# A bottleneck-attention block in fp32: four silus change places with the copies of the projection behind them

## The chip, the cores and the metric

The kernel runs on one core of a Trainium2 chip. The metric is the device time of one execution in microseconds, taken as the median of several runs. The core has five engines that each work through their own queue in order: TensorE (PE in the profile, with its weight loads apart as PEld), VectorE (DVE), ScalarE (ACT), GpSimd (POOL) and SyncE (SP, which issues DMAs). An instruction that has to wait for another engine waits on a semaphore, and everything behind it on its own queue waits with it.

## The reference

The input `x` has 8 samples of 512 channels of 32 x 32 pixels, in fp32. It is group-normed and sent through a block with two attention stages. The result is added to `x`. `cbs` is a convolution, a batch norm with fixed statistics and a silu.

```python
t = cbs(x, cv1_w, cv1_bn, 0)                     # 1x1, 512 -> 512
ys = [t[:, :C], t[:, C:]]                        # C = 256
for i in range(2):
    yi = ys[-1]
    z = cbs(yi, m_cv1_w[i], m_cv1_bn[i], 1)      # 3x3, 256 -> 256
    z = bot_attention(z, m_qkv_w[i], m_rw[i], m_rh[i])
    z = silu(bn_eval(conv2d(z, m_cv2_w[i], 0), m_cv2_bn[i]))
    ys.append(yi + z)
return cbs(concatenate(ys, axis=1), cv2_w, cv2_bn, 0)

def bot_attention(x, qkv_w, rw, rh):             # 4 heads of 64 channels, 1024 positions
    q, k, v = conv2d(x, qkv_w, 0) split in three
    logits = q . (k + rw + rh) * 64 ** -0.5
    return softmax(logits) . v
```

## The kernel before, in words

The eight samples are worked through in four pairs (loop variable `p`, 0 to 3). For each pair the program runs, stage by stage: the first 3x3 convolution (n = 0) on both samples together, then for each sample the projection to q, k and v and the attention, then the 1x1 convolution behind it; the same again with n = 1; and the closing 1x1 convolution. While the attention runs, pieces of the next pair's work are slipped in between. The order of the instructions on each engine is fixed when the program is built; `tc.issue_after(ins)` in the source ties an instruction behind another one of the same engine, and where no such tie stands a scheduler sets the order. Waits between engines are worked out from the tiles that instructions read and write.

**The 3x3 convolution** (`conv3x3`) is a Winograd transform. It runs over two blocks of 128 output channels (`oc`), and for each over three steps (`i`). In each step TensorE forms products into the PSUM tile `c3_ps` (L653), ScalarE copies part of them (L658), and VectorE turns them back into pixels. In the last step of the last block (`oc` = 1, `i` = 2), that VectorE work is cut in three parts: the first half of the pixels of the first sample, its second half, and the whole of the second sample. Each part ends with L714 and L715, which write the pixels into the tile `z`. Behind them stand silus on ScalarE (L719, recorded at L495), each in place on 512 pixels of `z`: one for the first part, one for the second, two for the third. I call these four **S1, S2, S3 and S4**. S1 makes the block called `b21` in the projection, S2 makes `b22`; S3 and S4 belong to the second sample, whose projection comes only after the first sample's attention.

**The projection** (`project_strassen`) forms q, k and v of one sample by seven products of blocks (Strassen-Winograd). A product is named by its weight: 11, s1, 12, s4, s2, s3, 22. Each has a part for q and k (L926, two matmuls of 512 columns, shown as x4 in the trace) and a part for v (L932, four matmuls of 128 columns, shown as x8). PSUM tiles collect them:

- product 11 (on `b11`) and product 12 (on `b21`) are summed in `ps_a` and in the first half of `ps_v`;
- product s1 (on `t1`) and product s4 (on `b22`) are summed in `ps_b` and in the second half of `ps_v`;
- s2 (on `t2`), s3 (on `t3`) and 22 (on `t4`) go to fresh tiles.

Before product 12 may be added onto product 11, the value of product 11 alone has to be saved, and the same for s1 and s4. That is what four ScalarE copies do: `u_z` (L968, from `ps_a`), `m_z` (L969, from `ps_b`), `u_zv` and `m_zv` (L971 and L972, from the two halves of `ps_v`). After products 12 and s4, five more copies bring out finished blocks: `q` and `vT` (L978, L980), then `kr`, `q` and `vT` (L983, L984, L985), and a table load for exp follows (L510), since the attention's exponentials come next on ScalarE. VectorE meanwhile makes `t2`, `t3`, `t4` from the blocks of `z` (L973 to L975), adds the position terms to k (L956), and later combines the products (L991 to L1016). The order of the matmuls on TensorE is 11 and s1 (q and k), 11 and s1 (v), 12 (q and k), 12 (v), s4 (q and k), s4 (v), s2, s3, 22, and then the attention's logits.

The tiles `q` and `kr` take over buffers that the convolution's VectorE work reads until its end (`c3_t` and `c3_k`, tags "q" and "k"), so their first writes wait for that work: the first `q` copy waits for L705 of the third part.

`project_strassen` is called with `table=True` right behind a convolution, for the first sample of a pair. This happens seven times: behind the convolution n = 0 of the pairs 1 to 3, and behind n = 1 of all four pairs. In pair 0 the first projection is another function (`project_direct`). The second sample's projections (`table` not set) have no convolution right ahead of them.

Of the kernel before, what the change touches and what calls it, by code (L numbers as in the profile page):

```python
# [61 lines left out]
def kernel(  # L62
# [16 lines left out]
    nc = tc.nc  # L79
# [5 lines left out]
    NM = C // P  # L85
# [8 lines left out]
    G = 2  # L94
# [396 lines left out]
    def stages(act, small, ps_big, ps_av, n_pt):  # L491
# [117 lines left out]

        def conv3x3(n, vs, u_of, z, groups=G, summed=None, after=None, between={}):  # L610

# [9 lines left out]
            for oc in range(NM):  # L621
                dst = z[:, oc].rearrange("p g x -> p (g x)").rearrange("p (t r w) -> p r t w", r=4, w=F)
                for i in range(NI):
# [57 lines left out]
                    for (at, size), m in zip(parts, m_parts):  # L681
# [31 lines left out]
                        if final:  # L713
                            stt(dst[:, 0, tl], tiles(r0), -6.0, tiles(big_s[:, xs_]), ALU.mult, ALU.add)  # L714
                            read = stt(dst[:, 3, tl], tiles(r1), -6.0, tiles(big_d[:, xs_]), ALU.mult, ALU.add)  # L715
                            for block in range(at // half_q, (at + size) // half_q):
                                g, half = divmod(block, NH)
                                z_part = z[:, oc, g, ts(half, HALF)]
                                last_silu = silu(z_part, z_part, bn_m1[n] + oc)  # L719
            if summed is None:  # L720
# [191 lines left out]

        def project_strassen(n, z, w, t, early=None, middle=None, table=False):

# [31 lines left out]
            def v_of(ap):  # L946
                return ap.rearrange("p (j o) -> p j o", o=P)
# [20 lines left out]
            nc.scalar.copy(u, ps_a)  # L968
            nc.scalar.copy(m5, ps_b)  # L969
            to_v(ps_v[:, 1], w["s1"], t1)  # L970
            nc.scalar.copy(u_v, ps_v[:, 0])  # L971
            nc.scalar.copy(m5_v, ps_v[:, 1])  # L972
            tt(t2, b22, t1, ALU.subtract)  # L973
# [10 lines left out]
            nc.scalar.copy(q1, ps_b[:, 0])  # L984
            copied = nc.scalar.copy(v1, v_of(ps_v[:, 1]))  # L985
            if table:
# [998 lines left out]
    for p in range(NP):  # L1985
        ia, ib = G * p, G * p + 1
        more = p + 1 < NP
        direct = p == 0
# [57 lines left out]
        def direct_keys(which):  # L2046
# [5 lines left out]
        }  # L2052
        z = new_z()
        t = s.conv3x3(
            0, vs, u_of(0), z, summed=None if direct else z[:, :, 0], after=last_out,
            between=in_first if direct else {},
        )
# [19 lines left out]
        else:  # L2077
            qkv = s.project_strassen(0, z[:, :, 0], take_blocks("sq", 0, 0, SQ_NAMES), t, table=True)

# [230 lines left out]
        z = new_z()  # L2310
        t = s.conv3x3(1, vs, u_of(1), z, summed=z[:, :, 0])
        feed(sqs(1, 1))
        w = take_blocks("sq", 1, 0, SQ_NAMES)
        qkv = s.project_strassen(1, z[:, :, 0], w, t, table=True)

# [269 lines left out]
```

## Time and profile before

| | |
|---|---|
| median of 3 runs | 2235.71 us (2235.07 to 2235.83) |
| the profiled execution | 2234.68 us, its span 2233.2 us |
| TensorE busy | 2192.9 us, 98% of the span |
| VectorE busy | 1752.3 us, 78% |
| ScalarE busy | 1094.0 us, 49% |
| GpSimd busy | 225.1 us, 10% |
| granted TensorE clock, mean | 0.998 of full speed |

The span is the time between the first and the last instruction in the trace; the device time has 1.5 us around it. In a row of the timeline stand the start in us from the span's start, the duration in us, the engine, the line, the operation, the tile written and the tiles read, the shapes and how many instructions are merged in the row. A bracket at the end gives the idle time of that engine just before the row and what ended it. Matmuls are pipelined: the next one starts a little before the row of the one ahead of it ends. ScalarE's and VectorE's instructions overlap in the same way by about 0.1 us.

The seven calls behind a convolution can be found by the start of their `u_z` copy: 374, 672, 923, 1219, 1468, 1764 and 1991 us. Of these 672, 1219 and 1764 stand behind n = 0, the other four behind n = 1.

### The profile page before, as it was taken

Reading aid. Unit: us, or ns where it says so; the run is one execution under the profiler, and the core shown is the slowest. Engines: PE = TensorE matmul, PEld = TensorE weight load, DVE = VectorE, ACT = ScalarE, POOL = GpSimd, SP = SyncE. Lnnn points to the kernel's source line nnn. Section 1 sums busy time; section 2 is a strip of 40 time slices with the busy share of each in tenths; the row PEclk is TensorE's granted clock in tenths of the full one; section 3 lists DMA queues with packets and bytes.
Section 4 is the critical chain, followed back from the end, with each engine's and each line's share of the span. In section 5 each row is a group of like instructions: output and inputs, shape, how many; then the busy total and the mean of one; then the engine's idle time right before and its main releaser. Section 6 shows DMA issues by size and latency. Waiting matters only on the chain.

```text
span 2233.2 us, 40366 instructions
## 1 busy us (share of the span) xinstructions
PE 2192.9 (98%) x16330; PEld 1079.5 (48%) x16330; DVE 1752.3 (78%) x2794; ACT 1094.0 (49%) x1324; POOL 225.1 (10%) x417
## 2 busy tenths in 40 slices
PE   7999999999999999999999999999999999999998
PEld 3653437343474444734447443564344834373433
DVE  7988879878669688986858868997794877897664
ACT  7554553644225666356323576445622455336543
POOL 3322210000220000000021000000002100000001
PEclk9999999999999999999999999999999999999999
DMA  9854447321582323612268141542126701251123
GB/s 271 307 170 140 162 149 258 109 74 52 141 256 73 103 97 121 209 49 77 58 155 272 34 156 44 180 140 77 58 67 170 267 30 44 91 202 39 58 58 96
DMA packets 133798, 285.61 MB, mean 128 GB/s; under 512 B 33540, under 2 KB 61184, under 8 KB 132580
## 3 DMA queue, kind: packets, MB, share of 16 engines
q1 hardware_dynamic: 101700, 197.34, 26.7%
q0 software_dynamic: 31904, 85.61, 13.2%
q8 instruction: 131, 2.15, 0.4%
q14 instruction: 63, 0.52, 0.1%
HBM read 214.86 MB, written 68.03 MB: 127 GB/s over the span
## 4 chain that ended last, share of the span: by engine, by line
PE 83%; DVE 12%; ACT 2%; issue 1%; DMA 1%; POOL 0%; SPq 0%; DVEq 0%; ACTq 0%; POOLq 0%
PE av_ps L1081 18%; PE l_ps L1047 17%; PE c L1315 9%; PE c_new L1315 8%; PE c_ps L653 8%; PE p_ps L926 5%; PE m_ps L1295 5%; PE x_ps L1555 4%; PE ps L523 3%; PE p_ps L932 3%; DVE acc L1067 2%; PE s_ps L1099 1%; PE p_ps L896 1%; DVE c_e L694 1%; DVE c_r L703 1%
## 5 line engine op out<-in xcount | busy, mean ns | idle before, releaser
L1051 ACT ACTIVATE pt<-l_ps 128x1024 f32<-128x1024 f32 x512 | 495.5, 1023 | 336.5 <-PE l_ps L1047 218.9
L1067 DVE TENSOR_TENSOR acc<-acc,pt 128x1024 f32<-128x1024 f32 x384 | 469.7, 1223 | 44.2 <-ACT pt L1051 17.2
L1081 PE MATMUL av_ps<-pt,vT 64*64 64x512 f32 x4096 | 484.9, 590 | 4.9 <-DVE z L1089 4.6
L1047 PE MATMUL l_ps<-q,kr 64*64 64x512 f32 x4096 | 486.1, 590 | 2.3 <-ACT pt L1051 1.2
L1081 PEld LDWEIGHTS av_ps<-pt,vT 64*64 64x64 f32 x4096 | 156.3, 133 | 284.4 <-issue 233.5
L1047 PEld LDWEIGHTS l_ps<-q,kr 64*64 64x64 f32 x4096 | 157.6, 133 | 272.2 <-issue 247.3
L653 PEld LDWEIGHTS c_ps<-v_in,u 128*64 128x64 f32 x4320 | 235.8, 137 | 6.4 <-issue 6.1
L653 PE MATMUL c_ps<-v_in,u 128*64 128x128 f32 x4320 | 238.6, 273 | 0.1
L1295 PE MATMUL m_ps<-z,m_sb 128*128 128x512 f32 x256 | 113.8, 592 | 0.0
L658 ACT COPY c_m<-c_ps 128x512 f32<-128x512 f32 x48 | 28.1, 585 | 166.7 <-PE c_ps L653 148.4
L1089 DVE TENSOR_TENSOR z<-av_ps,z 128x512 f32<-128x512 f32 x64 | 44.1, 690 | 80.6 <-ACT z L1088 80.6
L926 PE MATMUL p_ps<-t_z,sq 128*128 128x512 f32 x224 | 105.9, 595 | 0.0
L495 ACT ACTIVATE t<-m_ps,bh,sh 128x512 f32<-128x512 f32 x64 | 46.3, 774 | 93.8 <-PE m_ps L1295 92.6
L1065 DVE TENSOR_TENSOR acc<-pt 128x1024 f32<-128x1024 f32 x64 | 78.0, 1219 | 16.7 <-PE s_ps L1099 11.2
L926 PE MATMUL p_ps<-z,sq 128*128 128x512 f32 x168 | 81.0, 602 | 0.7 <-ACT z L495 0.7
L1295 PEld LDWEIGHTS m_ps<-z,m_sb 128*128 128x128 f32 x256 | 47.9, 190 | 56.5 <-issue 51.4
L495 ACT ACTIVATE z<-z,bh,sh 128x512 f32<-128x512 f32 x64 | 48.6, 806 | 36.3 <-DVE z L715 36.3
L1157 DVE TENSOR_TENSOR z<-z,rs 128x512 f32<-128x512 f32 x64 | 42.4, 687 | 25.2 <-DMA rs<-r_dram 25.1
L932 PEld LDWEIGHTS p_ps<-sq,z 128*128 128x128 f32 x336 | 43.3, 191 | 28.7 <-ACT m_zv L972 14.0
L926 PEld LDWEIGHTS p_ps<-t_z,sq 128*128 128x128 f32 x224 | 39.5, 191 | 36.5 <-issue 34.4
L1555 PE MATMUL x_ps<-t_x,sw 128*128 128x512 f32 x128 | 55.9, 592 | 0.0
L1315 PE MATMUL c_new<-t_in,wss 128*128 128x512 f32 x128 | 55.9, 592 | 0.0
(341 smaller groups left out, 3137.3 us busy)
## 6 DMA issues: line engine op xcount, KB each, us to landing
u<-u SPq DMA_DIRECT2D x135, 512.0 KB
y_in<-y SPq DMA_DIRECT2D x32, 512.0 KB
rs<-r_dram SPq DMA_DIRECT2D x126, 128.0 KB
sq<-sq SPq DMA_DIRECT2D x42, 384.0 KB
x<-in_x_dram SPq DMA_DIRECT2D x28, 512.0 KB
r_in<-r SPq DMA_DIRECT2D x28, 512.0 KB
c_out<-in_x_dram POOLq DMA_DIRECT2D x56, 256.0 KB, 5.1
out_dram<-c_out POOLq DMA_DIRECT2D x56, 256.0 KB, 3.7
```

Source lines behind the costliest of these rows:

```text
L495: silued[0] = nc.scalar.activation(dst, src, AF.Silu, scale=sh[:, k : k + 1], bias=bh[:, k : k + 1])
L653: conv_product[0] = nc.tensor.matmul(to[o], us[cp][:, k, row, c, o], rhs, start=(k == 0), stop=(k == NM - 1),)
L926: nc.tensor.matmul(ps[:, o, :], w[:, o, :], rhs, start=not onto, stop=True, skip_group_check=onto)
L932: nc.tensor.matmul(v[:, ts(j, P)], rhs[:, ts(j, P)], w[:, 2, :], start=j == 0 and not onto, stop=True, skip_group_check=True,)
L1047: nc.tensor.matmul(ps[kh * HD : (kh + 1) * HD, hd, :], kr[r, c, o : o + HD], q[r, c, ts(half, HALF)], start=True, stop=True,)
L1051: last_exp[0] = exp = nc.scalar.activation(pt, ps, AF.Exp, scale=SCALE)
L1065: return nc.vector.tensor_tensor(accs[g], pt[0], pt[1], ALU.add)
L1067: ins = nc.vector.tensor_tensor(accs[g], accs[g], pt[i], ALU.add)
L1081: nc.tensor.matmul(avs[g][hd * HD : (hd + 1) * HD, kh, :], vT[r, j, o : o + HD], pt[i][r, hd, :], start=(j == 0), stop=(j == NJ - 1),)
L1295: nc.tensor.matmul(pss[half][:, oc, :], m2_sb[:, n, k, ts(oc, P)], ao[:, k, ts(half, HALF)], start=(k == 0), stop=(k == NM - 1),)
L1315: nc.tensor.matmul(ps[:, o, :], w[:, k, ts(o, P)], rhs[part][:, c], start=(k == 0 and not onto), stop=(k == KB - 1), skip_group_check=onto,)
L1555: nc.tensor.matmul(ps[:, o, :], w[:, c, ts(o, P)], rhs[c], start=(c == 0 and not onto), stop=(c == 1), skip_group_check=onto,)
```

## The change

`conv3x3` gets a list, `silus`. In its last block of channels it no longer issues the four silus but puts them on the list. `project_strassen` takes them from there: S1 behind the copy `m_z`, S2 behind `m_zv`, S3 and S4 behind the last of the five copies and ahead of the table load. Each is tied behind the instruction named, and `u_zv` and `m_zv` are tied behind S1. Pair 0 with n = 0 is left as it was. Nothing is added or left out; the seven calls run the same instructions.

```diff
@@ conv3x3
-        def conv3x3(n, vs, u_of, z, groups=G, summed=None, after=None, between={}):
+        def conv3x3(n, vs, u_of, z, groups=G, summed=None, after=None, between={}, silus=None):
...
-                                last_silu = silu(z_part, z_part, bn_m1[n] + oc)
+                                if silus is not None and oc == NM - 1:
+                                    silus.append(lambda to=z_part, k=bn_m1[n] + oc: silu(to, to, k))
+                                else:
+                                    last_silu = silu(z_part, z_part, bn_m1[n] + oc)
@@ project_strassen
-        def project_strassen(n, z, w, t, early=None, middle=None, table=False):
+        def project_strassen(n, z, w, t, early=None, middle=None, table=False, silus=()):
+
+            def silus_behind(ins, n):
+                for _ in range(n if silus else 0):
+                    with tc.issue_after(ins.ins):
+                        ins = silus.pop(0)()
+                return ins
...
             nc.scalar.copy(u, ps_a)
-            nc.scalar.copy(m5, ps_b)
+            copied = silus_behind(nc.scalar.copy(m5, ps_b), 1)
             to_v(ps_v[:, 1], w["s1"], t1)
-            nc.scalar.copy(u_v, ps_v[:, 0])
-            nc.scalar.copy(m5_v, ps_v[:, 1])
+            with tc.issue_after(copied.ins):
+                nc.scalar.copy(u_v, ps_v[:, 0])
+                copied = nc.scalar.copy(m5_v, ps_v[:, 1])
+            silus_behind(copied, 1)
...
-            copied = nc.scalar.copy(v1, v_of(ps_v[:, 1]))
+            copied = silus_behind(nc.scalar.copy(v1, v_of(ps_v[:, 1])), 2)
             if table:
@@ the calls, for n = 0 (pairs 1 to 3) and n = 1 (all pairs)
+        silus = []
-            between=in_first if direct else {},
+            between=in_first if direct else {}, silus=None if direct else silus,
-            qkv = s.project_strassen(0, z[:, :, 0], take_blocks("sq", 0, 0, SQ_NAMES), t, table=True)
+            qkv = s.project_strassen(0, z[:, :, 0], take_blocks("sq", 0, 0, SQ_NAMES), t, table=True, silus=silus)
-        t = s.conv3x3(1, vs, u_of(1), z, summed=z[:, :, 0])
+        t = s.conv3x3(1, vs, u_of(1), z, summed=z[:, :, 0], silus=silus)
-        qkv = s.project_strassen(1, z[:, :, 0], w, t, table=True)
+        qkv = s.project_strassen(1, z[:, :, 0], w, t, table=True, silus=silus)
```

The first place is ScalarE's queue at the projection behind a convolution, from the first copy to the table load. The rows `z<-z` are S1, S2 and (x2) S3 with S4; `kr`, `q`, `vT` are the finished blocks. Before:

```order
L968 COPY u_z<-p_ps 128x1024
L495 ACTIVATE z<-z,bh,sh 128x512
L969 COPY m_z<-p_ps 128x1024
L495 ACTIVATE z<-z,bh,sh 128x512
L971 COPY u_zv<-p_ps 128x512
L972 COPY m_zv<-p_ps 128x512
L978 COPY q<-p_ps 128x512
L980 COPY vT<-p_ps 128x4x128
L495 ACTIVATE z<-z,bh,sh 128x512 x2
L983 COPY kr<-p_ps 128x512
L984 COPY q<-p_ps 128x512
L985 COPY vT<-p_ps 128x4x128
```

S1 stood ahead of `m_z`, S2 ahead of `u_zv` and `m_zv`, S3 and S4 ahead of `kr`. The same place with the change (line numbers grow by 9 to 11):

```order
L977 COPY u_z<-p_ps 128x1024
L978 COPY m_z<-p_ps 128x1024
L495 ACTIVATE z<-z,bh,sh 128x512
L981 COPY u_zv<-p_ps 128x512
L982 COPY m_zv<-p_ps 128x512
L495 ACTIVATE z<-z,bh,sh 128x512
L989 COPY q<-p_ps 128x512
L991 COPY vT<-p_ps 128x4x128
L994 COPY kr<-p_ps 128x512
L995 COPY q<-p_ps 128x512
L996 COPY vT<-p_ps 128x4x128
L495 ACTIVATE z<-z,bh,sh 128x512 x2
```

Now S1 stands behind `m_z`, S2 behind `m_zv`, and S3 with S4 behind the last `vT`; one table load follows them, as before.

The second place is VectorE's queue at the same point, where the third part of the convolution ends and `t2` is made. The rows `z<-c_r` are L714 and L715 of the third part, the row `t_z<-z,t_z` is `t2`. Before:

```order
L705 SCALAR_TENSOR_TENSOR c_r<-c_t,c_e 128x16x8
L973 TENSOR_TENSOR t_z<-z,t_z 128x512
L714 SCALAR_TENSOR_TENSOR z<-c_r,c_k 128x8x32
L715 SCALAR_TENSOR_TENSOR z<-c_r,c_k 128x8x32
L974 TENSOR_TENSOR t_z<-z 128x512
```

With the change:

```order
L705 SCALAR_TENSOR_TENSOR c_r<-c_t,c_e 128x16x8
L714 SCALAR_TENSOR_TENSOR z<-c_r,c_k 128x8x32
L715 SCALAR_TENSOR_TENSOR z<-c_r,c_k 128x8x32
L984 TENSOR_TENSOR t_z<-z,t_z 128x512
L985 TENSOR_TENSOR t_z<-z 128x512
```

`t2` has moved behind the two instructions that end the convolution. On TensorE, GpSimd and SyncE no instruction changes its place.

## The prediction

> **What bounds the kernel now.** I read the page first, for the engine that sets the time, and then the waits of that engine.
>
> ```profile
> PE 2192.9 (98%) x16330; PEld 1079.5 (48%) x16330; DVE 1752.3 (78%) x2794; ACT 1094.0 (49%) x1324; POOL 225.1 (10%) x417
> PE 83%; DVE 12%; ACT 2%; issue 1%; DMA 1%; POOL 0%; SPq 0%; DVEq 0%; ACTq 0%; POOLq 0%
> ```
>
> TensorE is busy for 98% of the span and holds 83% of the chain that ended last. A change that adds no matmul and takes none away can only gain what TensorE idles, some 40 us in all (2233.2 less 2192.9). So the view that counts is the list of TensorE's own waits (who waited for whom: total us, times, longest):
>
> ```profile
> PE p_ps L932 <- ACT m_zv L972: 5.8, 7, 1.0
> PE av_ps L1081 <- DVE z L1089: 4.6, 5, 1.6
> PE p_ps L926 <- ACT z L495: 0.7, 4, 0.2
> ```
>
> The first line is the place of the change: seven times, once in each call behind a convolution, the v part of product 12 waits for `m_zv`, 5.8 us in all. The third line is S1, for which the q and k part of product 12 waits. I then read the timeline of the first of the seven calls, engine by engine.
>
> ```profile
> 373.84 1.88 PE L926 MATMUL p_ps<-t_z,sq 128*128 128x512 f32 x4
> 376.45 1.06 PE L932 MATMUL p_ps<-sq,t_z 128*128 128x128 f32 x8
> 377.68 1.98 PE L926 MATMUL p_ps<-z,sq 128*128 128x512 f32 x4 [0.18 <-ACT z L495]
> 380.66 1.16 PE L932 MATMUL p_ps<-sq,z 128*128 128x128 f32 x8 [0.99 <-ACT m_zv L972]
> 381.66 1.88 PE L926 MATMUL p_ps<-z,sq 128*128 128x512 f32 x4
> 383.38 1.05 PE L932 MATMUL p_ps<-sq,z 128*128 128x128 f32 x8
> 384.27 1.88 PE L926 MATMUL p_ps<-t_z,sq 128*128 128x512 f32 x4
> ...
> 376.82 0.81 ACT L495 ACTIVATE z<-z,bh,sh 128x512 f32<-128x512 f32 x1 [1.76 <-DVE z L715]
> 377.54 0.99 ACT L969 COPY m_z<-p_ps 128x1024 f32<-128x1024 f32 x1
> 378.84 0.81 ACT L495 ACTIVATE z<-z,bh,sh 128x512 f32<-128x512 f32 x1 [0.31 <-DVE z L715]
> 379.56 0.56 ACT L971 COPY u_zv<-p_ps 128x512 f32<-128x512 f32 x1
> 380.02 0.59 ACT L972 COPY m_zv<-p_ps 128x512 f32<-128x512 f32 x1
> 381.17 0.59 ACT L978 COPY q<-p_ps 128x512 f32<-128x512 f32 x1 [0.56 <-DVE c_r L705]
> 385.37 1.28 ACT L510 ACT_TABLE_LOAD   x1
> 393.39 3.78 ACT L1051 ACTIVATE pt<-l_ps 128x1024 f32<-128x1024 f32 x4 [6.53 <-issue]
> ```
>
> Product s1's q and k part ends at 375.72 (373.84 + 1.88), and ScalarE stands idle for 1.76 us until S1 can run, although `m_z` could. Then S2 waits for VectorE, with `u_zv` and `m_zv` behind it: they run at 379.56 and 380.02, although their matmuls ended at 377.51 (376.45 + 1.06). `m_zv` ends at 380.61, and 0.05 us later TensorE goes on.
>
> **The change, part by part.** No instruction and no DMA is added or removed; silus, copies and one table load per call stay. Three moves count.
>
> **Copies ahead of silus, at the calls behind n = 1.** When may `m_z` start? The call for the second sample, where nothing stands ahead of the copies, tells:
>
> ```profile
> 451.36 1.98 PE L926 MATMUL p_ps<-t_z,sq 128*128 128x512 f32 x4
> 453.18 1.05 PE L932 MATMUL p_ps<-sq,z 128*128 128x128 f32 x8
> 454.07 1.06 PE L932 MATMUL p_ps<-sq,t_z 128*128 128x128 f32 x8
> 453.38 1.01 ACT L969 COPY m_z<-p_ps 128x1024 f32<-128x1024 f32 x1 [1.30 <-PE p_ps L926]
> 455.17 0.59 ACT L971 COPY u_zv<-p_ps 128x512 f32<-128x512 f32 x1 [0.77 <-PE p_ps L932]
> ```
>
> `m_z` starts 0.04 us after its matmuls (451.36 + 1.98 = 453.34) and takes 1.01. `u_zv` starts 0.04 after the *second* v part (455.13), though it reads only the first half of `ps_v`: the waits are for the whole tile. The rows also give the steps of TensorE without a wait: 1.82 from a q and k part that begins after other work or a gap to the next part (451.36 to 453.18; 1.72 in a running sequence, 381.66 to 383.38), and 0.89 from a v part (453.18 to 454.07), or 1.00 where that part begins after a gap (380.66 to 381.66).
>
> In the call at 374, then: `m_z` runs from 375.76 to 376.77. S1 can start at 376.82 as before, so product 12 starts at 377.68 as before and its 0.18 stays. `u_zv` and `m_zv` follow S1 and end at about 378.6. S2 finds ScalarE free at 378.84 and runs as before. The v part of product 12 now waits for nobody: 377.68 + 1.82 = 379.50 instead of 380.66. s4's q and k part follows at 380.39; it needs S2, which ended at 379.65. s4's v part could start at 382.11, and here something else is late. It writes `ps_v` and so needs the copy `vT` out of the other half, which stands behind `q`; and `q` starts at 381.17 whatever TensorE does, since it waits for L705 of VectorE. With 0.59 each and 0.1 of overlap, `vT` ends at 382.24, so s4's v part starts at 382.29 and s2 at 383.29. Before it was 384.27: a gain of 0.98. That the v part waits for `vT` is in the list of waits, for two calls of the second sample:
>
> ```profile
> PEld p_ps L932 <- ACT vT L980: 1.3, 2, 0.6
> ```
>
> The other three calls behind n = 1 have the same wait of 0.99 (the first and the last of the three), so I count four times 0.97, or 3.9 us:
>
> ```profile
> 929.36 1.16 PE L932 MATMUL p_ps<-sq,z 128*128 128x128 f32 x8 [0.99 <-ACT m_zv L972]
> ...
> 1997.16 1.16 PE L932 MATMUL p_ps<-sq,z 128*128 128x128 f32 x8 [0.99 <-ACT m_zv L972]
> ```
>
> **The same at the calls behind n = 0, where S1 was early.** Here TensorE had no gap at product 12, so `m_z` ahead of S1 costs something.
>
> ```profile
> 672.22 1.88 PE L926 MATMUL p_ps<-t_z,sq 128*128 128x512 f32 x4
> 678.54 1.16 PE L932 MATMUL p_ps<-sq,z 128*128 128x128 f32 x8 [0.94 <-ACT m_zv L972]
> 1218.43 1.88 PE L926 MATMUL p_ps<-t_z,sq 128*128 128x512 f32 x4
> 1223.97 1.16 PE L932 MATMUL p_ps<-sq,z 128*128 128x128 f32 x8 [0.16 <-ACT m_zv L972]
> 1763.96 1.88 PE L926 MATMUL p_ps<-t_z,sq 128*128 128x512 f32 x4
> 1770.05 1.16 PE L932 MATMUL p_ps<-sq,z 128*128 128x128 f32 x8 [0.70 <-ACT m_zv L972]
> ```
>
> From the end of the s1 row to product 12 it now takes 0.04 + 1.01 (`m_z`) - 0.09 (overlap) + 0.81 (S1) + 0.05 = 1.82. From product 12 to s2 it takes 1.82 + 0.89 + 1.72 + 0.89 = 5.32. Before, s2 came 3.61 after the v part in the row (380.66 to 384.27). So s2 starts at 674.10 + 7.14 = 681.24 instead of 682.15, at 1227.45 instead of 1227.58, and at 1772.98 instead of 1773.66: gains of 0.91, 0.13 and 0.68, together 1.7. `vT` does not hold s4 here; it is nearest at 672, where `q` (the row below) lets it end at 680.1, and s4's v part is due at 680.35.
>
> ```profile
> 679.05 0.59 ACT L978 COPY q<-p_ps 128x512 f32<-128x512 f32 x1 [0.56 <-DVE c_r L705]
> ```
>
> **S3 and S4 behind the last `vT`, and `t2` behind L715.**
>
> ```profile
> 381.00 0.68 DVE L973 TENSOR_TENSOR t_z<-z,t_z 128x512 f32<-128x512 f32 x1
> 381.94 0.42 DVE L715 SCALAR_TENSOR_TENSOR z<-c_r,c_k 128x256 f32<-128x256 f32 x1
> ```
>
> I cost both at nothing. At 374 the last `vT` would end at about 384.0, the two silus at 385.4, the table load at 386.7, as now (385.37 + 1.28). ScalarE is then idle for 6.53 us until the first logits are there; were that cover gone, the silus would cost their 1.5 us. `t2` trades places with L714 and L715, which end at 382.36 now (381.94 + 0.42); so `t2` ends there instead of at 381.68, and s2 asks for it at 383.29. With the cover gone that would be 0.7 per call.
>
> **Does the gain stay?** Behind s2, VectorE waits for TensorE before it combines the products, so its work moves ahead with TensorE's:
>
> ```profile
> 386.19 1.22 DVE L991 TENSOR_TENSOR u_z<-p_ps,u_z 128x1024 f32<-128x1024 f32 x1 [2.03 <-PE p_ps L926]
> 388.80 0.69 DVE L999 TENSOR_TENSOR kr<-p_ps,u_z 128x512 f32<-128x512 f32 x1 [0.79 <-PE p_ps L926]
> ```
>
> With 2.03 and 0.79 us of idle time there, everything that hangs on either engine starts earlier by the gain. **The sum** is 3.9 + 1.7 = 5.6 us: 2234.68 becomes 2229.1 for the profiled execution (span 2227.6). The median of the runs is 1.0 above it, so I forecast **2230.1 us**.
>
> The bounds. If no new wait arose at all, each call would go from product 12 to s2 without a stop: 1.27 at the four calls and 1.21, 0.43, 0.98 at the three, 7.7 in all. From below: a wide copy of 1024 columns lasts up to 1.10 (the row gives the shortest, the median and the longest in ns) instead of 1.01, which would delay S1 by 0.09 in seven calls, and 0.1 of start-up may be paid at four more places; that leaves 4.6.
>
> ```profile
> L968 ACT COPY u_z<-p_ps x14: 1012/1013/1095, 374.0 to 2067.0; 128x1024 f32<-128x1024 f32 x14
> ```
> I keep 5.6, since each duration in it is the row of the same instruction in the same place. The forecast's own range is 4.6 to 6.8 us of gain, 2228.9 to 2231.1.
>
> **The rivals.**
>
> *Waits by half tile.* If s4's v part did not wait for `vT`, the four calls would gain 0.29 more (0.18 + 0.11), in all 1.2: 2228.9. For it: the two halves are written and read apart. Against it: `u_zv` at 455.17 waited for the whole tile, and the weight load waited for `vT` above. [...] The rows of this case show the wider wait, so I do not take it.
>
> *The gain is eaten in the attention.* TensorE waits there for VectorE too (4.6 us in five waits, second line of the waits above), and VectorE holds 12% of the chain. If VectorE's work there does not move ahead, those waits grow by what TensorE won: up to all of 5.6, so 2235.7, or some 2233 where half is eaten. Against it stand the 2.03 and the 0.79 above.
>
> *Slower: `m_z` held back.* S1 now stands behind `m_z`. If `m_z` could start only when the v parts of 11 and s1 are through (377.51 instead of 375.72, 1.79 later), S1 and product 12 would be held with it. At 374, s2 would start at 377.51 + 7.14 = 384.65, 0.38 later than now; four such calls cost 1.5, the three others 1.79 less their gain, that is 0.88, 1.66 and 1.11: in all 5.2 us, **2240.9**. It decides from a delay of `m_z` of about 0.8 us (5.6 over 7). Against it stands 453.38, where `m_z` ran beside the v part.
>
> **How the numbers follow.** A change of 0.2%, 4.5 us, is about what a measurement of this kernel can tell from none. I give the forecast 0.69, the half-tile rival 0.08, the eaten gain 0.17, the slower case 0.06. The forecast lies 1.1 us beyond the bound of 4.5, and I count a tenth of it below: faster 0.62 + 0.08 = 0.70, the same 0.07 + 0.17 = 0.24, slower 0.06. The range reaches from somewhat below the half-tile case (2227.8) to a gain of which half is eaten (2233.2); the whole gain eaten and the slower case lie outside.
>
> **What would show it.** In the changed kernel's waits of TensorE the line for `m_zv` is gone; S1 still holds product 12 for 0.18 in four calls. The new waits for `vT` (four calls) and S1 (the three others) are to be read from starts, since a matmul's row runs 0.16 us into the next one's and hides most of them. `m_z` starts 0.04 after its matmuls; s2 starts 5.6 after product 12 at the n = 1 calls and 5.3 at the others, where product 12 starts 1.8 after the end of s1's q and k part. The first exponential still waits for logits. The forecast is wrong if `vT` or S1 holds TensorE for half a microsecond, or if TensorE's waits inside the attention have grown.

## The result and the profile after

The changed kernel takes **2229.14 us** (median of 12 runs, 2227.95 to 2230.16), against 2234.79 us for the kernel before (12 runs on the same chip): a ratio of 0.9976, with a 95% interval of 0.9968 to 0.9984. That is 5.65 us less, where 5.6 was forecast. The forecast time, 2230.1 us, is 1.0 us above the measured one. Run again beside other kernels, the change took 2229.32 us against 2233.99, 4.7 us less, ratio 0.9979 [0.9969, 0.9989]. The profiled execution has a span of 2227.6 us, as forecast. The first lines of its page, busy time and chain:

```profile
PE 2191.6 (98%) x16330; PEld 1078.3 (48%) x16330; DVE 1752.9 (79%) x2794; ACT 1094.5 (49%) x1324; POOL 224.5 (10%) x417
...
PE 87%; DVE 9%; ACT 1%; DMA 1%; issue 1%; SPq 0%; POOL 0%; DVEq 0%; ACTq 0%; POOLq 0%
```

What went is TensorE's idle time. From the first of the seven `u_z` copies to the end of the span TensorE is busy for 1837.1 us in both kernels, and its idle time there falls from 22.1 to 16.5 us. The two rows are the view by windows: the stretch, its length, then the busy time of TensorE, its weight loads, VectorE, ScalarE and GpSimd with their instructions, the granted clock, the DMA share and GB/s. The first is the kernel before.

```profile
374.04:2233.20 1859.16, 1837.09 (x13630) 892.16 (x13628) 1432.03 (x2164) 892.38 (x1034) 132.91 (x248) 1.00 0.35 111
373.93:2227.60 1853.67, 1837.15 (x13630) 892.57 (x13628) 1432.94 (x2164) 893.13 (x1034) 132.61 (x248) 1.00 0.35 111
```

That TensorE's busy time over the whole span is 1.3 us less than before (2191.6 against 2192.9) comes from the first convolution, where the trace before has 3.4 us at half clock (granted clock 0.50 from 77.37 to 80.78 us) and this one has none (1.00 there). The list of TensorE's own waits has no line for `m_zv` any more. These are the lines that answer to those of before, and one that has grown:

```profile
PE c_ps L653 <- DVE v_in L607: 5.4, 3, 2.8
PE av_ps L1092 <- DVE z L1100: 4.6, 5, 1.6
...
PE p_ps L935 <- ACT z L495: 0.7, 4, 0.2
```

The waits inside the attention (second line) are the 4.6 us they were, so nothing of the gain was eaten there. S1 still holds product 12 four times for 0.2. The first line belongs to the first convolution, at 76 to 101 us, which the change does not touch; it was 4.1 before and is between 3.1 and 5.6 in the kernels below. The start of the first of the seven calls varies by 1.7 us from trace to trace, so gains are read from there on. The waits of the weight loads show what took the place of `m_zv`:

```profile
PEld p_ps L941 <- ACT vT L991: 5.8, 9, 0.8
...
PEld p_ps L941 <- ACT m_zv L982: 2.4, 7, 0.5
PEld p_ps L935 <- ACT z L495: 2.1, 7, 0.4
```

Before, `vT` had 1.3 us there, and `m_zv` stood as follows:

```profile
PEld p_ps L932 <- ACT m_zv L972: 14.0, 14, 1.8
```

Now `vT` has 5.8 us in nine waits and S1 2.1 in seven. Most of these waits lie behind the matmuls ahead of them. The call at 374, with the start, the duration, and TensorE and ScalarE apart:

```profile
373.73 1.88 PE L935 MATMUL p_ps<-t_z,sq 128*128 128x512 f32 x4
...
377.57 1.99 PE L935 MATMUL p_ps<-z,sq 128*128 128x512 f32 x4 [0.17 <-ACT z L495]
379.39 1.05 PE L941 MATMUL p_ps<-sq,z 128*128 128x128 f32 x8
380.28 1.88 PE L935 MATMUL p_ps<-z,sq 128*128 128x512 f32 x4
382.18 1.16 PE L941 MATMUL p_ps<-sq,z 128*128 128x128 f32 x8
383.18 1.88 PE L935 MATMUL p_ps<-t_z,sq 128*128 128x512 f32 x4
...
375.65 1.01 ACT L978 COPY m_z<-p_ps 128x1024 f32<-128x1024 f32 x1 [0.70 <-PE p_ps L935]
376.70 0.81 ACT L495 ACTIVATE z<-z,bh,sh 128x512 f32<-128x512 f32 x1
...
377.92 0.59 ACT L982 COPY m_zv<-p_ps 128x512 f32<-128x512 f32 x1
378.72 0.81 ACT L495 ACTIVATE z<-z,bh,sh 128x512 f32<-128x512 f32 x1 [0.21 <-DVE z L715]
381.05 0.58 ACT L989 COPY q<-p_ps 128x512 f32<-128x512 f32 x1 [1.52 <-DVE c_r L705]
381.54 0.59 ACT L991 COPY vT<-p_ps 128x512 f32<-128x512 f32 x1
...
383.86 1.52 ACT L495 ACTIVATE z<-z,bh,sh 128x512 f32<-128x512 f32 x2
385.38 1.28 ACT L510 ACT_TABLE_LOAD   x1
...
392.30 3.77 ACT L1062 ACTIVATE pt<-l_ps 128x1024 f32<-128x1024 f32 x4 [5.43 <-issue]
```

`m_zv` ends at 378.51, long before the v part of product 12 that needs it (379.39). S2 runs at 378.72 (before 378.84), the table load behind S3 and S4 starts at 385.38 (before 385.37), and ScalarE still waits for the first logits. From product 12 to s2 it is 5.61 (377.57 to 383.18).

### The profile page after: what moved, and what is told of

Read it like the earlier page. It is cut to its first block, busy times and chain, and to the rows that moved or that the text cites. A ratio compares the mean times of both kernels' runs of the same rounds, so it can differ in the third digit from the quotient of the medians.

```text
span 2227.6 us, 40373 instructions
## 1 busy us (share of the span) xinstructions
PE 2191.6 (98%) x16330; PEld 1078.3 (48%) x16330; DVE 1752.9 (79%) x2794; ACT 1094.5 (49%) x1324; POOL 224.5 (10%) x417
## 4 chain that ended last, share of the span: by engine, by line
PE 87%; DVE 9%; ACT 1%; DMA 1%; issue 1%; SPq 0%; POOL 0%; DVEq 0%; ACTq 0%; POOLq 0%
PE av_ps L1092 18%; PE l_ps L1058 17%; PE c_ps L653 10%; PE c L1326 9%; PE c_new L1326 8%; PE p_ps L935 7%; PE m_ps L1306 5%; PE x_ps L1566 4%; PE ps L523 3%; PE p_ps L941 3%; DVE acc L1078 2%; PE s_ps L1110 1%; PE p_ps L899 1%; DMA ypad<-in_m_cv_w_dram 0%; PE pv_ps L941 0%
## 5 line engine op out<-in xcount | busy, mean ns | idle before, releaser
L495 ACT ACTIVATE c_out<-m_kept,bh,sh 128x512 f32<-128x512 f32 (+1 forms) x33 | 38.8, 1268 | 35.4 <-issue 15.2
```

The lines of the kernel that those rows point to most:

```text
L495: silued[0] = nc.scalar.activation(dst, src, AF.Silu, scale=sh[:, k : k + 1], bias=bh[:, k : k + 1])
```

## The experiments

Every kernel is compared with runs of the kernel before on the same chip, and read in two ways: by the medians, and by its trace. From the trace the table has the time from the end of s1's q and k part to the start of s2 in the seven calls (n = 1: 374, 923, 1468, 1991; n = 0: 672, 1219, 1764) and the sum of the seven gains; then the gain from the start of the first `u_z` copy (at 373 to 375 us) to the end of the span, which leaves the first stages out; and last the gain of the medians. All is in us, against the kernel before; a minus is slower.

| kernel | n = 1 calls, each | n = 0 calls, each | sum of gains | first `u_z` to end | medians |
|---|---|---|---|---|---|
| before | 8.54 to 8.55 | 8.04, 7.27, 7.81 | | | |
| the change | 7.56 to 7.57 | 7.13 to 7.14 | 5.6 | 5.5 | 5.7 |
| the change again | 7.56 to 7.57 | 7.13 to 7.14 | 5.7 | 5.8 | 4.7 |
| only S2 moves | 7.56 to 7.57 | 6.84 to 6.85 | 6.5 | 6.3 | 6.7 |
| only S1 moves | 8.53 to 8.55 | 7.89, 7.76, 7.93 | -0.4 | -0.3 | 0.1 |
| S3, S4 stay | 7.56 | 7.13 to 7.14 | 5.7 | 5.6 | 5.3 |
| change, `vT` ahead of `q` | 7.27 to 7.29 | 7.13 to 7.14 | 6.8 | 6.7 | 6.8 |
| the same, S1 early at n = 0 | 7.27 to 7.29 | 6.84 | 7.7 | 7.6 | 7.9 |
| `m_z` late | 11.08, 9.41, 11.09, 10.99 | 11.11, 9.41, 9.41 | -15.2 | -15.2 | -14.3 |
| `m_z` late, again | 11.08, 9.40, 11.09, 9.40 | 11.06, 9.41, 9.41 | -13.5 | -13.4 | -13.5 (1 run) |
| S1 behind `u_zv` | 8.49 to 8.50 | 8.49 to 8.50 | -2.1 | -2.2 | -2.5 |
| `m_z` last | 9.90, 11.29, 11.54, 11.57 | 9.89, 11.55, 11.55 | -20.0 | -20.0 | -20.4 (1 run) |

The sum over the seven calls and the time to the end agree within 0.3 us in every kernel: whatever TensorE wins or loses there goes whole into the span.

### The change again

The change itself, without an edit, beside two of the kernels below:

> The changed kernel itself, beside the two others of this call. Theory and rival alike: 5.6 us less than before, span 2227.6.

Measured: 2229.32 us against 2233.99, 4.7 us less by the medians, and 5.7 in the calls, against 5.6 the first time. The two intervals (0.9968 to 0.9984 and 0.9969 to 0.9989) agree; about 1 us of a gain is therefore not told by one pair of medians here, and the smaller differences below are read from the traces.

### Only S2 moves

S2 goes behind `m_zv`; S1 stays ahead of `m_z`, S3 and S4 ahead of `kr`. Against the change:

```diff
-            nc.scalar.copy(u, ps_a)
-            copied = silus_behind(nc.scalar.copy(m5, ps_b), 1)
+            copied = silus_behind(nc.scalar.copy(u, ps_a), 1)
+            with tc.issue_after(copied.ins):
+                copied = nc.scalar.copy(m5, ps_b)
...
-            nc.scalar.copy(v0, v_of(ps_v[:, 0]))
+            copied = silus_behind(nc.scalar.copy(v0, v_of(ps_v[:, 0])), 2)
...
-            nc.scalar.copy(k1, ps_b[:, 1])
+            with tc.issue_after(copied.ins):
+                nc.scalar.copy(k1, ps_b[:, 1])
...
-            copied = silus_behind(nc.scalar.copy(v1, v_of(ps_v[:, 1])), 2)
+            copied = nc.scalar.copy(v1, v_of(ps_v[:, 1]))
```

> Edit against the kernel before: of the four silus only S2 moves, behind m_zv; S1 stays ahead of m_z, S3 and S4 ahead of kr. Theory (S2's place is what counts, since m_zv waited behind S2 and S2 for VectorE): m_zv ends before the v part of product 12 is due in all seven calls. 0.97 at each of the four n = 1 calls (there s4's v part still waits for vT), and without S1 held up at n = 0 1.0, 0.43 and 0.98: 6.3 us less than before, 0.7 less than with the whole change, span 2226.9. Rival (the gain comes from m_z and so from S1's place): most of the 5.6 is missing, 0 to 2 us less than before.

Measured: 2228.05 us against 2234.70, ratio 0.9968 [0.9957, 0.9980]. By the median 6.7 us less, where 6.3 was expected. The span of its profiled execution, 2227.5, is 0.6 above the expectation: this execution reached its first call 0.6 us later than the kernel before (374.64 against 374.04), and from there on it gains 6.3. At the n = 0 calls TensorE now runs without a stop:

```profile
672.09 1.88 PE L935 MATMUL p_ps<-t_z,sq 128*128 128x512 f32 x4
...
675.60 1.88 PE L935 MATMUL p_ps<-z,sq 128*128 128x512 f32 x4
...
680.82 1.88 PE L935 MATMUL p_ps<-t_z,sq 128*128 128x512 f32 x4
```

Product 12 starts 1.63 after s1's q and k part ended (673.97) and s2 5.22 after it, against 1.82 and 5.32 with the change. At the n = 1 calls nothing differs from the change (7.56). So S2 carries all of the gain, and S1's move behind `m_z` takes back 0.3 in each n = 0 call.

### Only S1 moves

S1 goes behind `m_z`; S2 follows it, ahead of `u_zv`; S3 and S4 stay ahead of `kr`, by the same lines as in the last section, which are left out here. Against the change:

```diff
-            copied = silus_behind(nc.scalar.copy(m5, ps_b), 1)
+            copied = silus_behind(nc.scalar.copy(m5, ps_b), 2)
...
-            silus_behind(copied, 1)
...
```

> Edit against the kernel before: only S1 moves, behind m_z; S2 stays ahead of u_zv and m_zv, S3 and S4 ahead of kr. Theory: m_zv still ends behind S2, so the v part of product 12 starts where it did in all seven calls: no change, within 0.3 us of before, span 2233.2, and TensorE's wait for m_zv is still some 5 us in seven. Rival (m_z first is what helps): 4 to 5.6 us less than before.

Measured: 2234.61 us against 2234.70, ratio 1.0002 [0.9993, 1.0011]: no change, as expected. In its list of waits `m_zv` stands as before:

```profile
PE p_ps L941 <- ACT m_zv L982: 5.3, 7, 1.0
```

`m_z` is early here, but that alone frees nobody: S2, for which VectorE is late, still has `u_zv` and `m_zv` behind it. That the v part of product 12 starts where it did held for the n = 1 calls only; the n = 0 calls are 0.15 us shorter, 0.49 longer and 0.12 longer than before.

### S3 and S4 stay

The change, with S3 and S4 back ahead of `kr`:

```diff
-            nc.scalar.copy(v0, v_of(ps_v[:, 0]))
+            copied = silus_behind(nc.scalar.copy(v0, v_of(ps_v[:, 0])), 2)
...
-            nc.scalar.copy(k1, ps_b[:, 1])
+            with tc.issue_after(copied.ins):
+                nc.scalar.copy(k1, ps_b[:, 1])
...
-            copied = silus_behind(nc.scalar.copy(v1, v_of(ps_v[:, 1])), 2)
+            copied = nc.scalar.copy(v1, v_of(ps_v[:, 1]))
```

> Edit against the changed kernel: S3 and S4 go back ahead of kr, all else as changed. Theory (their place costs nothing either way): the last vT ends 1.5 us later, some 0.7 before product s3 asks for it; the same time as the changed kernel, within 0.3, 5.6 less than before. Rival (S3 and S4 ahead of kr hold back the copies that s3 needs, and their move is part of the gain): 1 us or more slower than the change, 0.15 at each call.

Measured: 2228.69 us against 2233.99, ratio 0.9978 [0.9968, 0.9987], beside 2229.32 for the change in the same group. In the calls the two agree to 0.01, so the move of S3 and S4 is worth nothing. `t2` still stands behind L715 in this kernel; its move was not run alone.

### `vT` ahead of `q`

The change, with the first `vT` copy ahead of the first `q` copy in the calls behind a convolution:

```diff
-            nc.scalar.copy(q0, ps_a[:, 0])
+            first = nc.scalar.copy(v0, v_of(ps_v[:, 0])) if table else None
+            with tc.issue_after(first.ins) if table else nullcontext():
+                nc.scalar.copy(q0, ps_a[:, 0])
...
-            nc.scalar.copy(v0, v_of(ps_v[:, 0]))
+            if not table:
+                nc.scalar.copy(v0, v_of(ps_v[:, 0]))
```

> Edit against the changed kernel: behind a convolution the first vT copy goes ahead of the first q copy (q waits for VectorE's L705). Theory (at the four n = 1 calls s4's v part waits for vT, and vT stands behind q): these four calls go from product 12 to s2 in 5.32 instead of 5.61, 0.29 each, 1.2 in all; 6.8 us less than before, span 2226.4. Rival (the 5.61 has another cause, such as a cold start of TensorE or S2): unchanged 5.61, 5.6 us less than before.

Measured: 2227.92 us against 2234.70, ratio 0.9970 [0.9959, 0.9981]; 6.8 us less, as expected.

```profile
377.10 1.98 PE L935 MATMUL p_ps<-z,sq 128*128 128x512 f32 x4 [0.17 <-ACT z L495]
378.92 1.05 PE L941 MATMUL p_ps<-sq,z 128*128 128x128 f32 x8
379.81 1.88 PE L935 MATMUL p_ps<-z,sq 128*128 128x512 f32 x4
381.53 1.05 PE L941 MATMUL p_ps<-sq,z 128*128 128x128 f32 x8
382.43 1.88 PE L935 MATMUL p_ps<-t_z,sq 128*128 128x512 f32 x4
...
380.01 0.59 ACT L989 COPY vT<-p_ps 128x512 f32<-128x512 f32 x1 [0.95 <-PE p_ps L941]
380.53 0.59 ACT L991 COPY q<-p_ps 128x512 f32<-128x512 f32 x1
```

With `vT` starting at 380.01, s4's v part follows its q and k part in 1.72 instead of 1.90, and s2 comes 5.33 after product 12 instead of 5.61. So it was `vT`, held behind `q`, that stood in the way of s4's v part. The 0.28 in each of four calls is what the prediction took off for it.

### S1 early at n = 0 as well

The kernel of the last section, with S1 ahead of `m_z` in the n = 0 calls, where it is early, and behind it in the others:

```diff
+            copied = nc.scalar.copy(u, ps_a)
+            if n == 0:
+                copied = silus_behind(copied, 1)
+            with tc.issue_after(copied.ins):
+                copied = nc.scalar.copy(m5, ps_b)
+            if n == 1:
+                copied = silus_behind(copied, 1)
```

> Edit against the changed kernel: vT ahead of q as in the run before this one, and S1 ahead of m_z at the n = 0 calls only (behind m_z at n = 1). Theory: no new wait is left; the three n = 0 calls gain 1.21, 0.43 and 0.98 over before, the four others 1.27 each: 7.7 us less than before, 2.1 less than the change, span 2225.5. Rival (what is won further is eaten elsewhere, in the attention): the same time as the changed kernel, 5.6 less than before.

Measured: 2226.82 us against 2234.70, ratio 0.9964 [0.9950, 0.9977]; 7.9 us less, where 7.7 was expected. It has the lowest median of all. Against the changed kernel its calls are 2.0 us shorter together. The intervals of the two (up to 0.9977 here, from 0.9968 there) overlap, so that this difference rests on the traces and not on the times.

### The slower rival made real: `m_z` late

The change with `u_zv` ahead of `m_z` in the calls behind a convolution, so that `m_z`, and S1 behind it, wait for the v parts, and for `u_zv` too, which the rival did not have:

```diff
-            copied = silus_behind(nc.scalar.copy(m5, ps_b), 1)
-            to_v(ps_v[:, 1], w["s1"], t1)
+            if table:
+                to_v(ps_v[:, 1], w["s1"], t1)
+                copied = nc.scalar.copy(u_v, ps_v[:, 0])
+                with tc.issue_after(copied.ins):
+                    copied = silus_behind(nc.scalar.copy(m5, ps_b), 1)
+            else:
+                copied = nc.scalar.copy(m5, ps_b)
+                to_v(ps_v[:, 1], w["s1"], t1)
             with tc.issue_after(copied.ins):
-                nc.scalar.copy(u_v, ps_v[:, 0])
+                if not table:
+                    nc.scalar.copy(u_v, ps_v[:, 0])
                 copied = nc.scalar.copy(m5_v, ps_v[:, 1])
```

> Edit against the changed kernel: behind a convolution u_zv goes ahead of m_z, so that m_z and S1 behind it wait for the second v part; the slower rival made real. Theory (what ScalarE holds back ahead of S1 comes out of TensorE one for one): product 12 starts 2.31 after the v part of s1 ends, and s2 5.32 later. Against before 0.87 more at each n = 1 call, and 1.37, 2.15 and 1.60 at n = 0: 8.6 us more than before, span 2241.8. Rival (a delay of this size is taken up again in the attention): within 2 us of before.

Measured: 2248.33 us against 2233.99, ratio 1.0064 [1.0047, 1.0080]: 14.3 us slower, not 8.6. The profiled execution, at 2250.03 us, is the slowest of the four (the others 2247.66 to 2248.88), and its calls lose 15.2. The waits came out as worked out (seven times 2.30):

```profile
PE p_ps L935 <- ACT z L495: 16.1, 7, 2.3
```

What was missing is TensorE's speed behind the wait. The row is product 12's q and k part in the call at 1991 us (2003 in this kernel), which takes 3.57 instead of 1.98; behind it stand the windows of that call and of the call at 923 (928 in this kernel), where the part takes 1.98:

```profile
2009.00 3.57 PE L935 MATMUL p_ps<-z,sq 128*128 128x512 f32 x4 [2.30 <-ACT z L495]
```

```profile
2009.00:2012.30 3.30, 3.30 (x4) 1.51 (x5) 3.27 (x10) 1.13 (x2) 0.00 (x0) 0.51 0.10 41
934.20:937.50 3.30, 3.30 (x14) 2.10 (x15) 3.27 (x10) 2.11 (x4) 0.00 (x0) 1.00 0.19 66
```

The second fence is the view by windows again. In the first stretch the granted clock is 0.51 and TensorE gets no further than these four matmuls; in the second, behind the same wait of 2.30 us, it is 1.00 and ten more follow (14). Four of the seven calls are hit (374, 672, 1468, 1991) and come out at 11.0 to 11.1 instead of 9.41. Four times 1.6 to 1.7 are the 6.6 us that the expectation lacked in this execution.

### Which wait costs the clock

Three kernels were run on this question. In the first, S1 stands behind `u_zv`, and `m_z` is on time:

```diff
-            copied = silus_behind(nc.scalar.copy(m5, ps_b), 1)
+            copied = nc.scalar.copy(m5, ps_b)
...
-                nc.scalar.copy(u_v, ps_v[:, 0])
+                copied = silus_behind(nc.scalar.copy(u_v, ps_v[:, 0]), 1)
+            with tc.issue_after(copied.ins):
                 copied = nc.scalar.copy(m5_v, ps_v[:, 1])
```

> The change, with S1 behind u_zv instead of behind m_z (m_z stays second, m_zv and S2 follow). u_zv starts 1.82 us after the end of s1's q and k part, as in the kernel with m_z late; S1 0.48 later, so product 12 starts 3.17 us after that end and TensorE stands idle for 1.38 us in each of the seven calls (2.30 with m_z late, nothing to 0.17 in the change). s2 follows 5.32 later, 8.49 us after that end in all seven, against 8.55 before in four calls and 8.04, 7.27 and 7.81 in the three others: 2.1 us slower than before. This is to tell what the 2.30 us gaps paid beyond their waiting. Theory (only a long gap costs the clock): after 1.38 us no call runs its next matmuls slowly, and the kernel is 2.1 us slower than before. Rival (any gap behind a convolution may cost the clock): four calls of seven again lose 1.6, some 6.6 us more, 8.7 slower than before.

Measured: 2236.83 us against 2234.33, ratio 1.0012 [1.0002, 1.0021]: 2.5 us slower, and 2.1 by the calls.

```profile
377.79 1.98 PE L935 MATMUL p_ps<-z,sq 128*128 128x512 f32 x4 [1.39 <-ACT z L495]
```

Behind seven waits of 1.39 us no call runs slowly. In the second kernel `u_zv` and `m_zv` both stand ahead of `m_z`:

```diff
-            copied = silus_behind(nc.scalar.copy(m5, ps_b), 1)
-            to_v(ps_v[:, 1], w["s1"], t1)
-            with tc.issue_after(copied.ins):
-                nc.scalar.copy(u_v, ps_v[:, 0])
-                copied = nc.scalar.copy(m5_v, ps_v[:, 1])
+            if table:
+                to_v(ps_v[:, 1], w["s1"], t1)
+                copied = nc.scalar.copy(u_v, ps_v[:, 0])
+                with tc.issue_after(copied.ins):
+                    copied = nc.scalar.copy(m5_v, ps_v[:, 1])
+                with tc.issue_after(copied.ins):
+                    copied = silus_behind(nc.scalar.copy(m5, ps_b), 1)
...
```

> The change, with u_zv and m_zv both ahead of m_z and S1 behind it. m_z starts 0.48 us later than in the kernel with m_z late, so product 12 starts 4.57 us after the end of s1's q and k part and TensorE stands idle for 2.78 us in each of the seven calls. s2 follows 5.32 later, at 9.89: slower than before by 4 times 1.34 and by 1.85, 2.62 and 2.08, 11.9 us in all, and to that 1.65 for each call whose next matmuls run at the low clock. Theory (the longer the gap, the more calls are hit): more than the four calls of seven that were hit at 2.30 us, five to seven, so 20 to 23.5 us slower than before. Rival (which calls are hit has to do with the call, not with the gap's length): the same four calls, at 374, 672, 1468 and 1991 us, 18.5 slower.

Measured, in one run: 2254.69 us against 2234.33, 20.4 us slower. Five of the seven calls are hit behind waits of 2.79 us; those at 374 and 672, which were hit with `m_z` late, are not, and 923, 1219 and 1764 are. The call thus does not decide. That a longer wait hits more calls is not shown by five of seven against four of seven. The third kernel is that with `m_z` late once more:

> The kernel with m_z late once more, unchanged. Its waits are fixed by the order: 2.30 us of idle TensorE in each of the seven calls, 8.6 us slower than before. Theory (whether the clock falls depends on when the gap begins, against something that runs on its own): another set of calls, of another number, is hit by 1.65 each. Rival (it depends on the call): the calls at 374, 672, 1468 and 1991 us again and no others, 15.2 us slower.

Measured, in one run: 2247.80 us, 13.5 us slower. Now three calls are hit, 374, 672 and 1468; the one at 1991 no longer is, with the same wait:

```profile
680.38 3.64 PE L935 MATMUL p_ps<-z,sq 128*128 128x512 f32 x4 [2.30 <-ACT z L495]
...
2008.59 1.98 PE L935 MATMUL p_ps<-z,sq 128*128 128x512 f32 x4 [2.30 <-ACT z L495]
```

Three calls were hit in both executions, and the one at 1991 in one of them only: the same call of the same kernel, behind the same wait, is hit or not. The last section shows what differs.

## Why the prediction was right

**The place of the loss.** The line of `m_zv`, 5.8 us in TensorE's waits, was the right one to start from, and the seven calls are 5.6 us shorter together. Calls without any stop would have gained 7.7, the prediction's upper bound; the rest is missing for the two reasons that the prediction gave, `vT` behind `q` (1.2) and S1 behind `m_z` at n = 0 (0.9).

**Calls behind n = 1, forecast 4 times 0.97 to 0.98.** Product 12 starts as late as before (1.96 behind s1, before 1.96) because S1 waits for VectorE. From there to s2 it is 5.60 or 5.61 in all four, worked out as 5.61. The named next limit, `vT` behind `q` behind VectorE's L705, was the real one: with `vT` moved ahead it went away and left the 0.29 that had been worked out. Gained: 4 times 0.98.

**Calls behind n = 0, forecast 0.91, 0.13 and 0.68.** Product 12 starts 1.81 behind s1's end, worked out as 1.82, and s2 follows after 5.32.

```profile
1215.52 1.88 PE L935 MATMUL p_ps<-t_z,sq 128*128 128x512 f32 x4
...
1219.21 1.98 PE L935 MATMUL p_ps<-z,sq 128*128 128x512 f32 x4
...
1224.53 1.88 PE L935 MATMUL p_ps<-t_z,sq 128*128 128x512 f32 x4
...
1217.43 1.01 ACT L978 COPY m_z<-p_ps 128x1024 f32<-128x1024 f32 x1 [0.70 <-PE p_ps L935]
1218.34 0.81 ACT L495 ACTIVATE z<-z,bh,sh 128x512 f32<-128x512 f32 x1
```

S1 (1218.34 to 1219.15) now stands behind `m_z` and lets product 12 go 0.06 later. The gains are 0.91, 0.13 and 0.67. The prediction had charged these calls for S1 behind `m_z`: without that its bound has 1.21, 0.43 and 0.98, and with S2 alone the gains are 1.20, 0.43 and 0.97. What it did not say is that S1's move wins nothing anywhere, since the n = 1 calls are as short without it.

**S3, S4 and `t2` at nothing.** For S3 and S4 this is shown by the kernel in which they stay. For `t2` there are the rows alone: in the call at 374 it ends at 382.36, and s2, which needs it, starts at 383.18. The cover of S3 and S4, ScalarE's idle time ahead of the first exponential, was 6.53 and is 5.43 now: it shrank by what TensorE won, but it is far from gone.

**The gain stays.** VectorE's wait ahead of the first combination was the argument.

```profile
381.68 0.68 DVE L984 TENSOR_TENSOR t_z<-z,t_z 128x512 f32<-128x512 f32 x1
...
385.09 1.23 DVE L1002 TENSOR_TENSOR u_z<-p_ps,u_z 128x1024 f32<-128x1024 f32 x1 [0.93 <-PE p_ps L935]
...
387.70 0.69 DVE L1010 TENSOR_TENSOR kr<-p_ps,u_z 128x512 f32<-128x512 f32 x1 [0.79 <-PE p_ps L935]
```

The wait ahead of L1002 was 2.03 and is 0.93 (the first row is `t2`): VectorE ends its own work at the same point and waits 1.1 us less. That also says how far this can go on in these calls: with another 0.9 us won at s2, VectorE would be the one that is late. The waits in the attention stayed at 4.6, and the rival of the eaten gain fell with them.

**The time, and the hundredths.** The forecast time added 1.0 us to the profiled execution, from a median of three runs. Over 12 runs the median lies 0.1 above that execution (2234.79 against 2234.68), so this term was too large by 0.9 us, and the forecast time with it. The gain by the calls came out at 5.6 and 5.7 in two traces. That the medians, too, differ by 5.65 is partly luck: the second pair of medians gave 4.7.

**The rivals.** The half-tile rival fell at the row of s4's v part, 1.90 behind its q and k part and not 1.72. Its price of 1.2 was right, since that is what moving `vT` brought. The waits of this program are laid by whole tiles, here as before the change, and what laying them by half tile could win at this place is these 1.2 us. The slower rival did not come to pass, because `m_z` starts 0.04 after its matmuls (375.65 behind 375.61). Its price was reckoned from the waits alone, though. The kernels that make such a wait real show that a longer one, of 2.30 us, cost the clock too in 7 of 14 calls. Its wait would have been 1.82 us long, between the 1.39 that never cost it and those 2.30; that length was not tried. In the last section 1.83 us of idle time in one window left the clock full and 1.98 did not, so its price of 5.2 probably held.

## What to carry to other kernels

An instruction that waits here is charged with what stands behind it on its queue: three copies that were ready had stood behind silus that were not (`m_z` behind S1, started 1.82 us after its matmuls ended, `u_zv` and `m_zv` behind S2, 2.05 and 2.51 after theirs, in the call at 374), and moving the one silus that mattered (S2) brought all of the gain, while the move of S1, made for the same reason, cost a little wherever S1 had not been late. So decide such a move call by call, from the row in which each of the two becomes ready, and look at once for what is late next (here `vT` behind `q`), since that sets how much of the old wait comes back. A wait on a busy TensorE was not always worth only its length: here seven of 14 waits of 2.30 us cost another 1.6 to 1.7 us in clock.

## What the runs showed of the hardware

Behind seven of 14 waits of 2.30 us in the middle of an otherwise full TensorE its clock was half of full speed (0.51 in the row of the call at 1991 above), which the expectation of 8.6 us left out. The rows, for `m_z` last: two stretches in succession behind a wait, and the same stretch in a call that was not hit.

```profile
1484.60:1488.00 3.40, 3.39 (x4) 1.51 (x5) 3.37 (x9) 0.66 (x1) 0.00 (x0) 0.51 0.06 22
1488.10:1491.40 3.30, 3.30 (x20) 2.34 (x19) 0.69 (x1) 1.68 (x4) 0.00 (x0) 1.00 0.00 0
380.30:383.70 3.40, 3.40 (x14) 2.11 (x15) 3.37 (x10) 1.72 (x3) 0.00 (x0) 1.00 0.04 13
```

The granted clock falls to one half for 3.41 us, product 12's four matmuls of 512 columns then take up to 3.64 us instead of 1.98, and a hit costs 1.4 to 1.7 us (1.4 at 923 with `m_z` last, where, by an estimate from the missing 0.3 us at half clock, some 0.6 us of the slow stretch fell into the wait itself). Seven of 14 waits of 2.30 us and five of 7 of 2.79 us were hit, and none of the seven of 1.39. The slow stretch need not begin with the first matmul: in the call at 1764 with `m_z` last it ended at 1788.34 us, so it began at 1784.93, 1.4 us after product 12 did (1783.50), which took 2.40 there.

The slow stretches need not begin where a wait ends, and their ends keep one spacing. In the trace of the kernel before, the one in the first convolution ends at 80.78 us and the clock falls again, as the program ends, at 2227.76. One length of 3.41 us, that of the stretch, goes 629 times into the 2146.98 us between them if it is 3.4133. By the granted clock, the slow stretches in the trace of `m_z` late (a first one lies in the first convolution, as in the kernel before) end at 80.27, 384.05, 684.43, 1486.56 and 2012.21 us. Divided by 3.4133 us, the distances from the first are 89.0, 177.0, 412.0 and 566.0. In the second execution of that kernel the ends are 79.60, 383.38, 683.75 and 1485.89, with the same distances of 89.0, 177.0 and 412.0. With `m_z` last, where the calls stand at other distances, the ends are 935.00, 1235.38, 1487.96, 1788.34 and 2017.03, with 88.0, 162.0, 250.0 and 317.0. The quotients come out whole; what keeps the spacing is not shown.

On this spacing the idle time of TensorE can be read in windows of 3.41 us. Here is the call at 1991 in both executions of `m_z` late, each with the window of the wait and the window behind it:

```profile
2005.39:2008.80 3.41, 1.30 (x12) 1.11 (x10) 3.41 (x18) 2.07 (x3) 0.00 (x0) 1.00 0.32 100
2008.80:2012.21 3.41, 3.21 (x4) 1.52 (x5) 3.38 (x11) 1.33 (x3) 0.00 (x0) 0.50 0.14 54
...
2004.71:2008.12 3.41, 1.58 (x15) 1.39 (x13) 3.41 (x19) 1.79 (x3) 0.00 (x0) 1.00 0.25 53
2008.13:2011.54 3.41, 2.95 (x13) 1.95 (x14) 3.38 (x11) 2.22 (x5) 0.00 (x0) 1.00 0.28 108
```

The wait is 2.30 us in both. In the first, the edge between two windows comes late in the wait: 2.11 us of idle time fall into one window, and the next has half the clock. In the second the edge comes earlier, 1.83 us fall into one window, and the clock stays. The traces of the kernel before and of the change can be cut up in the same way, from the first full clock in their records, at some 16 us, to where the clock falls as the program ends. Here is the window with the most idle time in each, with the one behind it, before and then with the change:

```profile
73.95:77.37 3.42, 1.21 (x22) 1.24 (x24) 3.39 (x10) 1.65 (x4) 1.82 (x5) 1.00 1.03 412
77.37:80.78 3.41, 3.41 (x36) 3.41 (x34) 3.31 (x9) 0.00 (x0) 0.00 (x0) 0.50 1.04 413
...
74.34:77.75 3.41, 1.66 (x31) 1.69 (x33) 3.38 (x12) 1.17 (x4) 1.81 (x5) 1.00 1.02 413
77.75:81.17 3.42, 3.42 (x64) 3.23 (x62) 3.31 (x7) 0.59 (x1) 0.00 (x0) 1.00 1.05 419
```

Before, 2.21 us are followed by half the clock, and the next most, 1.63 us, are not; with the change the most is 1.75 us, and the clock stays. The wait of 2.79 us at 374 with `m_z` last, which was not hit, is cut by an edge at 378.63 us (counted back from 935.00) into 1.15 and 1.64 us. The wait of 2.79 us at 1764, which was hit, is cut by the edge at 1781.52 (one window ahead of 1784.93) and has 1.98 us behind it. So in the windows given here the most idle time that left the clock full is 1.83 us, and the least with half the clock behind it 1.98. This was read from the traces afterwards and no kernel was built to try it; the ends of matmuls are modelled, so its hundredths should not be trusted.
